# Attention sums over keys: from wide TensorE products to VectorE transpositions, and reciprocals broadcast through DRAM

## The chip, the cores and the metric

The kernel runs on one NeuronCore of one Trainium2 chip. The time is the device time of one execution in microseconds (us). Engines are named as in the profile: PE is TensorE (matrix products; PEld its weight loads), DVE is VectorE, ACT is ScalarE, POOL is GpSimd, SP is SyncE, which here only issues DMAs. A lower time is better.

## The reference

Four layers follow one another on x of shape (4, 512, 32, 32) in float32, each as x = x + f(group_norm(x)): an attention with mixed heads, a small simulated circuit that gates channels, an ordinary attention, and a lookup of the 8 best of 2048 memory rows. The change is in the third of them, layer 2:

```
q = conv1x1(x, Wq);  k, v = split(conv1x1(x, Wkv))        # 8 heads of 64 channels, 1024 positions
attn = softmax(einsum('bhct,bhcs->bhts', q, k) * 64**-0.5) # over the keys s
out  = conv1x1(einsum('bhts,bhcs->bhct', attn, v), Wp)
```

There are 4 images, so 4 x 8 heads x 1024 queries, each with a sum over 1024 keys. The kernel takes the softmax without subtracting a maximum, and so at its end it looks at a flag: if any reciprocal of a sum in layers 0 and 2 lay outside 1e-18 to 1e12, a second, general path computes everything anew.

## The kernel before

Layer 2 goes image by image. In an image, the eight heads are four pairs (m), the queries two halves of 512 (n), the keys eight tiles of 128. A *unit* is one pair of heads with one half of the queries; there are 8 an image, 32 in all. `UNITS2` lists half units (m, n, t0), t0 being 0 or 4, the first of four key tiles.

`scores2` computes a half unit. For each of four key tiles, PE multiplies keys and queries of the two heads (L1013) into a PSUM tile `sc` of 128 keys x 2 heads x 512 queries. ACT takes exp of it (L1007) into one of six places in `eT`. POOL adds pairs of these tiles (L1027 for the first pair, which starts the sum `es`; L1031 for the others), and DVE adds each such pair to `es` (L1032). `es` then holds, for 128 rests of the key index, partial sums over the eight tiles.

Between the second and the fourth exp, `scores2` calls `apply2` for the half unit before: PE multiplies values with the exponentials (L1046) and gathers the products of the eight tiles in a bank `pv`. Where `apply2` begins a unit (t0 == 0) it calls `finish2` for the unit that ended just before. `finish2` lets PE sum `es` over the partitions: two products of a matrix of ones with 512 columns, one for each head, which leave each sum in 64 partitions (L1067). ACT copies the result to SBUF (L1072), DVE takes 128x512 reciprocals (L1073) and multiplies `pv` by them into `o` (L1074). SP copies one row of reciprocals for each head into `seen` (L1077), which is looked at near the end (L1424).

At the end of an image the queries of the next image are projected, then the last half unit is applied, then the keys of the next image, then `finish2`, the values, the first scores of the next image, and `put_out2`, which projects `o` and adds x. After the last image comes one tile of layer 3's products (`attention`, L1134) in place of the next image's work.

PSUM has three `sc` buffers of two banks, which scores, small products and the sums of `finish2` take in turn, and two `pv` banks. Matrix products stand in program order (`pin`); instructions that aren't pinned are placed by the scheduler of the tile framework, each engine and each DMA queue then working in its own order.

Layer 0 has a similar step for its own sums (`sums`, L547 to L560): a product of a 128x128 matrix `same` with 32 columns of sums, a 128x32 reciprocal, two counting instructions into `seen0` (L552), a DMA of 32 rows to DRAM (`r_rows`, L556) and two DMAs from there, each broadcast to 64 partitions (L560).

Of the kernel before, what the change touches and what calls it, by code (L numbers as in the profile page):

```python
# [10 lines left out]
F32 = mybir.dt.float32  # L11
AF = mybir.ActivationFunctionType
ALU = mybir.AluOpType
AX = mybir.AxisListType
PSUM = bass.MemoryType.PSUM

P = 128
B = 4
C = 512
T = 1024  # L20
KC = C // P
TC = T // P
NB = 512
NH = 8
HD = C // NH
GSZ = C // 32
QB = 2
NQ = 9
# [8 lines left out]
R_LO, R_HI = 1e-18, 1e12  # L37
# [4 lines left out]
def fast_net(ctx: ExitStack, tc: tile.TileContext, a: dict, out: bass.AP, flag: bass.AP):  # L42
    nc = tc.nc
# [3 lines left out]
    const = ctx.enter_context(tc.tile_pool(name="const", bufs=1))  # L47
    small = ctx.enter_context(tc.tile_pool(name="small", bufs=4))
# [7 lines left out]
    def pin(ins):  # L56

        return tc.keep_in_program_order(ins)
# [5 lines left out]
    def chan(src, name):  # L64
# [11 lines left out]
    bp2 = chan(a["bp"], "bp2")  # L76
    fcb = chan(a["fc_b"], "fcb")

    both = const.tile([P, C], F32, tag="fcw", name="fcw")
    fcw, seen = both[0:NQ], both[HD:P]  # L80
    nc.scalar.dma_start(out=fcw, in_=a["fc_w"])
    qpar = const.tile([P, NL * NQ], F32, tag="qpar", name="qpar")
    nc.scalar.dma_start(out=qpar, in_=a["q_params"].partition_broadcast(P))
# [5 lines left out]
    ones = const.tile([P, P], F32, tag="ones", name="ones")  # L89
# [8 lines left out]
        out=gavg_v, in_=gavg_v, compare_op=ALU.is_ge, fill=0.0, base=0,  # L98
# [3 lines left out]
        out=gavg_v, in_=gavg_v, compare_op=ALU.is_ge, fill=0.0, base=GSZ - 1,  # L102
        pattern=[[GSZ, P // GSZ], [0, GSZ]], channel_multiplier=-1,
    )
    NS = 32
# [5 lines left out]
    same = const.tile([P, P], F32, tag="same", name="same")  # L111
# [119 lines left out]
    img = [dict() for _ in range(B)]  # L231
# [746 lines left out]
    def take_k2(b, m, at=None):  # L978
        I = img[b]
        if m == 0:  # L980
            I["k"] = big("k", f"k2_{b}")
        project(I["Wk"], tokens(I["xn"]), m, at, lambda ps: pin(nc.scalar.activation(
            I["k"][:, m, :], ps, AF.Identity, bias=bk2[:, m:m + 1])), f"k2_{b}")
# [11 lines left out]
    def scores2(b, u, before=None):  # L995

        m, n, t0 = u
        I = img[b]  # L1000
        nm = f"c{b}_{m}_{n}"
        es, scs = [], []

        def exp2():
            e = places2[:, count[0] % 6]
            count[0] += 1
            pin(nc.scalar.activation(e, scs[len(es)], AF.Exp))  # L1007
            es.append(e)

        for i, t in enumerate(range(t0, t0 + 4)):  # L1010
            sc = ps_s.tile([P, 2, NB], F32, tag="sc", name=f"sc_{nm}_{t}")
            for r in range(2):
                pin(nc.tensor.matmul(  # L1013
                    sc[:, r, :],
                    I["k"][r * HD:(r + 1) * HD, m, t * P:(t + 1) * P],
                    I["q"][r * HD:(r + 1) * HD, m, n * NB:(n + 1) * NB],
                    start=True, stop=True,
                ))
            scs.append(sc)
            if before is None or i < 2:  # L1020
                exp2()
        if before is not None:
            apply2(b, before, exp2)
        I["e", u] = list(es)
        if t0 == 0:
            I["es", m, n] = sums2[:, (2 * m + n) % 2]
            nc.gpsimd.tensor_add(I["es", m, n], es[0], es[1])  # L1027
            es = es[2:]
        for i in range(0, len(es), 2):
            two = pair_sum[:, (t0 + i) // 2 % 2]  # L1030
            nc.gpsimd.tensor_add(two, es[i], es[i + 1])  # L1031
            nc.vector.tensor_add(I["es", m, n], I["es", m, n], two)  # L1032

    def apply2(b, u, exp2=None):

        m, n, t0 = u
        I = img[b]
        if t0 == 0:
            finish2(b)
            I["pv", m, n] = ps_m.tile([P, NB], F32, tag="mm", name=f"pv_c{b}_{m}_{n}")  # L1040
        pv = I["pv", m, n]
        for i, e in enumerate(I.pop(("e", u))):
            t = t0 + i
            for r in range(2):
                h = 2 * m + r
                pin(nc.tensor.matmul(  # L1046
                    pv[r * HD:(r + 1) * HD, :], I["v"][:, t, h * HD:(h + 1) * HD],
                    e[:, r, :], start=(t == 0), stop=(t == TC - 1),
                ))
            if exp2 and i < 2:  # L1050
                exp2()
        if t0 == TC - 4:
            I["due"] = (m, n)

    def finish2(b):
        I = img[b]
        due = I.pop("due", None)
        if due is None:
            return
        m, n = due  # L1060
        nm = f"c{b}_{m}_{n}"
        if due == (0, 0):
            I["o"] = o_full.rearrange("p (k t) -> p k t", k=KC)
        es, pv = I.pop(("es", m, n)), I.pop(("pv", m, n))
        rsp = ps_s.tile([P, 2, NB], F32, tag="sc", name=f"rs_{nm}")[:, 0, :]
        for r in range(2):
            pin(nc.tensor.matmul(  # L1067
                rsp[r * HD:(r + 1) * HD, :], ones[:, 0:HD], es[:, r, :],
                start=True, stop=True,
            ))  # L1070
        ri = apool.tile([P, NB], F32, tag="rb", bufs=2, name=f"ri_{nm}")
        nc.scalar.copy(ri, rsp)  # L1072
        nc.vector.reciprocal(ri, ri)  # L1073
        nc.vector.tensor_mul(I["o"][:, m, n * NB:(n + 1) * NB], pv, ri)  # L1074
        for r in range(2):
            i = 2 * ((b * KC + m) * (T // NB) + n) + r
            nc.sync.dma_start(out=seen[i:i + 1, :], in_=ri[r * HD:r * HD + 1])  # L1077

    def put_out2(b):
        I = img[b]  # L1080
# [41 lines left out]
            ))  # L1122
            yield

    def attention(b, tt):

        nm = f"{b}_{tt}"
        att = eight_k([P, NI], f"att_{nm}")
        for half in range(2):
            sc = ps_s.tile([P, T], F32, tag="sc", name=f"at_{nm}_{half}")  # L1130
            for n in range(T // NB):
                i0 = half * T + n * NB
                for k in range(KC):
                    pin(nc.tensor.matmul(  # L1134
                        sc[:, n * NB:(n + 1) * NB],
                        xn3[b][:, k, tt * P:(tt + 1) * P], memT[k][:, i0:i0 + NB],
                        start=(k == 0), stop=(k == KC - 1),
                    ))
            pin(nc.scalar.copy(att[:, half * T:(half + 1) * T], sc))  # L1139
        return att  # L1140

    def pick(b, tt, att):
# [212 lines left out]
    for k in range(KC):  # L1355
        if k < 2:
            m_ = apool.tile([P, NI], F32, tag="s2", bufs=2, name=f"memT{k}")
        else:
            m_ = eT_flat[:, (4 + k) * NI:(5 + k) * NI]
        nc.sync.dma_start(out=m_, in_=a["memT"][k * P:(k + 1) * P, :])  # L1360
        memT.append(m_)
    tiles = [(b, tt) for b in range(B) for tt in range(TC)]
    atts, picks, sums = {}, {}, {}
    scores2(0, UNITS2[0])
    for b in range(B):
        last = b + 1 == B
        behind = chain(
            behind if b else state["behind"], norm3(b - 1) if b > 0 else gating(B - 1))
        ahead = prepare3(0) if last else prepare2(b + 1)
        for s, u in enumerate(UNITS2):  # L1370
            if s == 5 and not last:
                load2(b + 1)
            if s == 5 and last:
                img[b]["Wp"] = load_w("Wp", f"Wp2_{b}")
            if s >= 1:
                scores2(b, u, UNITS2[s - 1])
            for _ in range(2):
                if s >= 3:
                    next(behind, None)
                if s >= 8:  # L1380
                    next(ahead, None)
        run_out(ahead)
        if not last:
            for m in range(KC):
                take_q2(b + 1, m)
            img[b]["Wp"] = load_w("Wp", f"Wp2_{b}")
        apply2(b, UNITS2[-1])
        if not last:
            for m in range(KC):
                take_k2(b + 1, m)  # L1390
        finish2(b)
        if last:
            atts[0] = attention(*tiles[0])
        else:
            for i in range(TC // 2):
                take_v2(b + 1, i)
            scores2(b + 1, UNITS2[0])
        put_out2(b)
# [18 lines left out]
            next(behind, None)  # L1417


    counts = small.tile([P, 3], F32, tag="counts", name="counts")  # L1420
    nc.vector.memset(counts, 0.0)
    passed = apool.tile([P, NB], F32, tag="xr", bufs=2, name="passed")[HD:P]
    for i, (bound, op) in enumerate(((R_LO, ALU.is_ge), (R_HI, ALU.is_le))):
        nc.vector.tensor_scalar(  # L1424
            passed, seen, bound, None, op, ALU.add, accum_out=counts[HD:P, i:i + 1]
        )
    nc.vector.tensor_reduce(counts[:, 2:3], seen0, AX.X, ALU.add)
    tot = small.tile([P, 1], F32, tag="tot", name="tot")
    nc.vector.tensor_reduce(tot, counts, AX.X, ALU.add)
    tps = ps_m.tile([P, NB], F32, tag="mm", name="tot")  # L1430
    nc.tensor.matmul(tps[:, 0:1], ones, tot, start=True, stop=True)
    nc.vector.tensor_scalar(
        flag, tps[0:1, 0:1], float(2 * HD * NB + 2 * P * NS * B * TC), None, ALU.not_equal)


@with_exitstack
# [702 lines left out]
```

## Time and profile before

| what | value |
| --- | --- |
| median of 3 runs | 2636.74 us (2635.33 to 2646.7) |
| profiled execution: its own time, and its span | 2636.8 us, 2635.1 us |
| PE, DVE, POOL, ACT busy | 97%, 57%, 45%, 38% of the span |
| sums over keys on PE (L1067) | 128 records, about 604 ns each (they overlap) |
| ACT copies of the sums (L1072) | 32 of 0.586 us |
| reciprocals (L1073) | 32 of 3.346 us |
| multiplications by them (L1074) | 32 of about 0.68 us |
| pair sums on POOL (L1031) | 96 of 2.414 us |
| adds of pair sums on DVE (L1032) | 96 of 1.315 us |

A row such as `L1073 DVE RECIPROCAL ri_c<-ri_c 128x512 f32<-128x512 f32` names the line, the engine, the operation, the tile written and the tile read (shared buffers have the name of the first tile in them, so `eT` stands for several), and their shapes. A float32 product appears as two records, and records of PE overlap, so their durations don't add up; the distance between starts does. What stands in brackets at the end of a timeline row is how long the engine was idle before it, and what released it.

### The profile page before, as it was taken

Reading aid. Unit: us, or ns where it says so; the run is one execution under the profiler, and the core shown is the slowest. Engines: PE = TensorE matmul, PEld = TensorE weight load, DVE = VectorE, ACT = ScalarE, POOL = GpSimd, SP = SyncE. Lnnn points to the kernel's source line nnn. Section 1 sums busy time; section 2 is a strip of 40 time slices with the busy share of each in tenths; the row PEclk is TensorE's granted clock in tenths of the full one; section 3 lists DMA queues with packets and bytes.
Section 4 is the critical chain, followed back from the end, with each engine's and each line's share of the span. In section 5 each row is a group of like instructions: output and inputs, shape, how many; then the busy total and the mean of one; then the engine's idle time right before and its main releaser. Section 6 shows DMA issues by size and latency. Waiting matters only on the chain.

```text
span 2635.1 us, 47129 instructions
## 1 busy us (share of the span) xinstructions
PE 2553.4 (97%) x18350; PEld 1158.9 (44%) x18350; DVE 1498.8 (57%) x2451; ACT 997.3 (38%) x1148; POOL 1196.3 (45%) x1699
## 2 busy tenths in 40 slices
PE   8999999999999999999999999999999999999995
PEld 3344434554355534545533433443343344444442
DVE  4499338970789338871354145234413547788786
ACT  1566236651666236651252145025314622121210
POOL 2266315552456425552283056017404617656664
PEclk9999999999999999999999999999999999999997
DMA  2478439871698338793300220030012036767665
GB/s 81 129 218 236 107 101 228 251 201 54 176 256 243 104 96 222 226 248 120 128 1 17 71 73 1 32 128 1 1 53 75 1 100 184 221 183 219 187 181 156
DMA packets 182360, 349.82 MB, mean 133 GB/s; under 512 B 32361, under 2 KB 95849, under 8 KB 178418
## 3 DMA queue, kind: packets, MB, share of 16 engines
q1 hardware_dynamic: 100896, 167.17, 21.0%
q0 software_dynamic: 49152, 142.79, 19.9%
q10 hardware_dynamic: 32082, 36.76, 5.2%
q8 instruction: 148, 2.42, 0.4%
q14 instruction: 82, 0.67, 0.1%
HBM read 178.57 MB, written 33.69 MB: 81 GB/s over the span
## 4 chain that ended last, share of the span: by engine, by line
PE 87%; DMA 6%; DVE 3%; ACT 2%; issue 1%; SPq 1%; POOL 0%; ACTq 0%; POOLq 0%; DVEq 0%
PE at L1134 17%; PE pair L193 10%; PE sc_c L1013 9%; PE pv_c L1046 9%; PE pv L523 7%; PE pair L458 6%; PE pair L484 5%; PE pt L417 4%; DMA s<-ss 4%; PE p L193 3%; PE pt L711 3%; PE k L193 3%; PE v L205 3%; PE q L193 3%; ACT e L491 1%; PE rs_c L1067 1%
## 5 line engine op out<-in xcount | busy, mean ns | idle before, releaser
L473 POOL DMA_DIRECT2D s<-ss x512 | 258.9, 512 | 456.8 <-PE pair L484 154.9
L497 DVE STREAM_TRANSPOSE eT<-e 128x1024 f32<-128x1024 f32 x256 | 316.4, 1236 | 206.0 <-ACT e L491 205.6
L1151 POOL DMA_INDIRECT got<-in_mem,ix x256 | 277.9, 1086 | 217.5 <-DVE tmx L1157 94.3
L512 DVE BATCH_NORM_STATS2 st<-e 128x6 f32<-128x256 f32 x1024 | 350.4, 403 | 6.2 <-POOL sqs L571 6.2
L1007 ACT ACTIVATE eT<-sc_c 128x1024 f32<-128x1024 f32 x256 | 247.7, 1022 | 276.0 <-PE sc_c L1013 213.8
L491 ACT ACTIVATE e<-pair 128x1024 f32<-128x1024 f32 x256 | 251.7, 1022 | 187.9 <-PE pair L484 136.2
L1031 POOL TENSOR_TENSOR e<-eT 128x1024 f32<-128x1024 f32 x96 | 231.7, 2414 | 179.2 <-ACT eT L1007 153.9
L464 ACT COPY ss<-pair 128x1024 f32<-128x1024 f32 x256 | 247.3, 1019 | 87.4 <-PE pair L458 43.2
L458 PE MATMUL pair<-k,q 64*32 64x512 f32 x4096 | 265.1, 598 | 11.8 <-ACT e L491 11.8
L1032 DVE TENSOR_TENSOR eT<-eT,e 128x1024 f32<-128x1024 f32 x96 | 126.3, 1315 | 247.5 <-POOL e L1031 247.2
L523 PE MATMUL pv<-eT,v 128*64 128x128 f32 x4096 | 252.0, 276 | 5.9 <-ACT pv L583 5.9
L523 PEld LDWEIGHTS pv<-eT,v 128*64 128x64 f32 x4096 | 222.2, 137 | 76.1 <-issue 56.9
L1013 PE MATMUL sc_c<-q,k 64*128 64x512 f32 x1024 | 237.2, 602 | 2.6 <-DVE xr L674 2.3
L1027 POOL TENSOR_TENSOR eT<-eT 128x1024 f32<-128x1024 f32 x32 | 81.0, 2533 | 344.4 <-ACT eT L1007 334.2
L1046 PE MATMUL pv_c<-eT,v 128*64 128x512 f32 x1024 | 232.2, 596 | 0.0
L484 PE MATMUL pair<-s,wmix 32*32 32x512 f32 x4096 | 159.7, 606 | 14.8 <-DMA s<-ss 8.9
L1175 DVE SCALAR_TENSOR_TENSOR acc<-got,et,acc 128x512 f32<-128x512 f32 x224 | 168.5, 752 | 8.0
L1073 DVE RECIPROCAL ri_c<-ri_c 128x512 f32<-128x512 f32 x32 | 107.1, 3346 | 96.1 <-ACT ri_c L1072 96.1
L1013 PEld LDWEIGHTS sc_c<-q,k 64*128 64x128 f32 x1024 | 93.5, 186 | 131.8 <-issue 72.0
L1139 ACT COPY att<-at 128x1024 f32<-128x1024 f32 x64 | 64.8, 1012 | 216.6 <-PE at L1134 216.5
L1046 PEld LDWEIGHTS pv_c<-eT,v 128*64 128x64 f32 x1024 | 70.3, 137 | 152.8 <-issue 152.2
L458 PEld LDWEIGHTS pair<-k,q 64*32 64x32 f32 x4096 | 57.6, 105 | 172.9 <-ACT e L491 79.5
(290 smaller groups left out, 3279.5 us busy)
## 6 DMA issues: line engine op xcount, KB each, us to landing
s<-ss SPq DMA_DIRECT2D x512, 128.0 KB
s<-ss POOLq DMA_DIRECT2D x512, 128.0 KB, 4.8
rb<-r POOLq DMA_DIRECT2D x64, 128.0 KB, 6.6
o<-o SPq DMA_DIRECT2D x32, 256.0 KB
xr<-in_x ACTq DMA_DIRECT2D x32, 256.0 KB
x<-xr SPq DMA_DIRECT2D x32, 256.0 KB
xr_c<-x SPq DMA_DIRECT2D x32, 256.0 KB
x<-xr_c SPq DMA_DIRECT2D x32, 256.0 KB
```

The source lines that it names most:

```text
L193: pin(nc.tensor.matmul(ps[:, n, :], w[:, k, m * P:(m + 1) * P], rhs(k, n), start=(k == 0), stop=(k == KC - 1),))
L458: pin(nc.tensor.matmul(sc[m * NS:(m + 1) * NS, r, :], q[r * HD:(r + 1) * HD, m, s * NS:(s + 1) * NS], k_[r * HD:(r + 1) * HD, m, n * NB:(n ...
L473: pin(relays[side].dma_start(out=s2[2 * m + r::NH], in_=ss[m * NS:(m + 1) * NS, r, :]))
L484: pin(nc.tensor.matmul(mixed(s, r // 2)[t * NS:(t + 1) * NS, r % 2, :].rearrange("p (qq k) -> p qq k", qq=2), wmix[r * NS:(r + 1) * NS], s ...
L491: pin(nc.scalar.activation(e[:, half].rearrange("p r qq k -> p (r qq k)"), flat2(mixed(s, half)), AF.Exp))
L497: pin(nc.vector.transpose(eT[:, j % 2].rearrange("p b (qq i r) x -> p i r qq b x", qq=2, i=4)[:, i, 2 * half:2 * half + 2], e[:, half].rea ...
L512: pin(nc.vector.bn_stats(st[:, i, 2 * half + r, qq, :], e[:, half, r, qq, :]))
L523: pin(nc.tensor.matmul(pv[r * HD:(r + 1) * HD, gp, :], I["v"][:, t, g * HD:(g + 1) * HD], eT[:, j % 2, t, :, 4 * g:4 * g + 4], start=(t == ...
L1013: pin(nc.tensor.matmul(sc[:, r, :], I["k"][r * HD:(r + 1) * HD, m, t * P:(t + 1) * P], I["q"][r * HD:(r + 1) * HD, m, n * NB:(n + 1) * NB] ...
L1046: pin(nc.tensor.matmul(pv[r * HD:(r + 1) * HD, :], I["v"][:, t, h * HD:(h + 1) * HD], e[:, r, :], start=(t == 0), stop=(t == TC - 1),))
L1134: pin(nc.tensor.matmul(sc[:, n * NB:(n + 1) * NB], xn3[b][:, k, tt * P:(tt + 1) * P], memT[k][:, i0:i0 + NB], start=(k == 0), stop=(k == K ...
L1151: pin(nc.gpsimd.indirect_dma_start(out=got[:, i, :], out_offset=None, in_=a["mem"], in_offset=bass.IndirectOffsetOnAxis(ap=ix[:, i:i + 1], ...
```

## The change

The sum over the 128 partitions is moved from PE mostly to DVE. When a unit's `es` is complete (at the end of `scores2`, t0 == 4), the new `over_keys` turns `es` in blocks of 32x32 (two transpositions of 128x512) and adds 32 neighbours (two reductions to 128x16). What remains, a sum over four groups of partitions, is made by two small products with `same`, which was layer 0's matrix and is scaled by POOL once. They stand in `invert2`, at the place where `finish2` stood. `invert2` also takes 128x32 reciprocals straight from PSUM, turns them, counts them into `seen0`, and sends them through DRAM, on POOL's queue, to a 128x512 tile `rb`. `finish2` is now only the multiplication of `pv` by `rb`, and stands half a unit later. At an image's end, `invert2` comes after the first of the four key projections; after the last image, between the two halves of the first `attention` tile. The tile `seen`, its DMAs and its counting go.

```diff
@@ scores2
+        if t0 == TC - 4:
+            over_keys(b, m, n)
@@ apply2
         if t0 == 0:
+            invert2(b)
+            I["pv", m, n] = ps_m.tile([P, NB], F32, tag="mm", name=f"pv_c{b}_{m}_{n}")
+        else:
             finish2(b)
-            I["pv", m, n] = ps_m.tile([P, NB], F32, tag="mm", name=f"pv_c{b}_{m}_{n}")
@@
+    def over_keys(b, m, n):
+        I = img[b]
+        es = I.pop(("es", m, n))
+        s_ = I["s", m, n] = small.tile([P, 2, NB // NS], F32, tag="sums", name=f"s_c{b}_{m}_{n}")
+        for r, tag in enumerate(("o1", "xs")):
+            turned = apool.tile([P, NB], F32, tag=tag, name=f"est_{b}_{m}_{n}_{r}")
+            nc.vector.transpose(turned, es[:, r, :])
+            nc.vector.tensor_reduce(
+                s_[:, r, :], turned.rearrange("p (q x) -> p q x", x=NS), AX.X, ALU.add)
+
+    def invert2(b):
...
+        m, n = I["ready"] = due
+        ps = ps_s.tile([P, 2, NB], F32, tag="sc", name=f"rs_{nm}")[:, 0, 0:NS]
+        s_ = I.pop(("s", m, n)).rearrange("p r q -> p (r q)")
+        for half in range(2):
+            pin(nc.tensor.matmul(
+                ps[half * HD:(half + 1) * HD], same[:, half * HD:(half + 1) * HD], s_,
+                start=True, stop=True))
+        ri = small.tile([P, NS], F32, tag="ri", name=f"ri_c{nm}")
+        nc.vector.reciprocal(ri, ps)
+        ris = small.tile([P, NS], F32, tag="ssq", name=f"ris_{nm}")
+        nc.vector.transpose(ris, ri)
+        for bound, op in ((R_LO, ALU.is_ge), (R_HI, ALU.is_le)):
+            nc.vector.scalar_tensor_tensor(seen0, ri, bound, seen0, op, ALU.add)
+        rows = r_rows[n % 2]
+        nc.gpsimd.dma_start(out=rows, in_=ris[0:NS])
+        rb = I["rb", m, n] = apool.tile([P, NB], F32, tag="rb", bufs=2, name=f"rb_c{nm}")
+        for r in range(2):
+            nc.gpsimd.dma_start(
+                out=rb[r * HD:(r + 1) * HD],
+                in_=rows.rearrange("(r q) x -> r (q x)", r=2)[r].partition_broadcast(HD))
+
     def finish2(b):
...
-        for r in range(2):
-            pin(nc.tensor.matmul(
-                rsp[r * HD:(r + 1) * HD, :], ones[:, 0:HD], es[:, r, :],
-                start=True, stop=True,
-            ))
-        ri = apool.tile([P, NB], F32, tag="rb", bufs=2, name=f"ri_{nm}")
-        nc.scalar.copy(ri, rsp)
-        nc.vector.reciprocal(ri, ri)
-        nc.vector.tensor_mul(I["o"][:, m, n * NB:(n + 1) * NB], pv, ri)
-        for r in range(2):
-            i = 2 * ((b * KC + m) * (T // NB) + n) + r
-            nc.sync.dma_start(out=seen[i:i + 1, :], in_=ri[r * HD:r * HD + 1])
+        nc.vector.tensor_mul(
+            I["o"][:, m, n * NB:(n + 1) * NB], I.pop(("pv", m, n)), I.pop(("rb", m, n)))
@@ before layer 2
+    nc.gpsimd.tensor_scalar_mul(same, same, 8.0 / T)
@@ at the end of an image
             for m in range(KC):
                 take_k2(b + 1, m)
+                if m == 0:
+                    invert2(b)
+        if last:
+            atts[0] = attention(*tiles[0], lambda: invert2(b))
         finish2(b)
@@ at the end
-        nc.vector.tensor_scalar(
-            passed, seen, bound, None, op, ALU.add, accum_out=counts[HD:P, i:i + 1]
-        )
...
-        flag, tps[0:1, 0:1], float(2 * HD * NB + 2 * P * NS * B * TC), None, ALU.not_equal)
+        flag, tps[0:1, 0:1], float(2 * P * NS * B * (TC + 2 * KC)), None, ALU.not_equal)
```

## The prediction

> **What bounds the kernel now.** I read the page first: its busy shares, and the chain that ended last, by engine and by line.
>
> ```profile
> span 2635.1 us, 47129 instructions
> PE 2553.4 (97%) x18350; PEld 1158.9 (44%) x18350; DVE 1498.8 (57%) x2451; ACT 997.3 (38%) x1148; POOL 1196.3 (45%) x1699
> ...
> PE 87%; DMA 6%; DVE 3%; ACT 2%; issue 1%; SPq 1%; POOL 0%; ACTq 0%; POOLq 0%; DVEq 0%
> ```
>
> TensorE is the bound over the whole span, so an edit is worth what it takes from or adds to PE's row of products. Layer 2 runs from about 1290 to 2163 us. Table of windows there, in stretches of one unit (15.5 us): PE is busy 15.50 in nearly every one, DVE 5 to 13, ACT 8.5, POOL 9.4 to 14.3, at a granted clock of 1.00; DMA is 0.00 to 0.01 while units run. Next the chain in order of time, where the products stand one after the other (start, us, what):
>
> ```profile
> 1303.41 3.63 PE sc_c L1013 x16
> 1307.05 3.58 PE pv_c L1046 x16
> 1310.63 3.63 PE sc_c L1013 x16
> 1314.27 1.01 PE rs_c L1067 x4
> 1315.27 3.43 PE pv_c L1046 x16
> ...
> 1330.57 3.43 PE pv_c L1046 x16
> 1334.00 0.32 PE gps_b L146 x2
> ```
>
> A unit is twice (scores, values); the sums over keys, rs_c, come in the middle and take 1.01. The values product takes 3.58 where the scores follow, 3.43 where something else does: a change of operand form costs 0.15. So rs_c is worth 1.01 - 0.15 = 0.86 us a unit. The timeline of one unit shows the side engines (start, busy us, engine, line):
>
> ```profile
> 2097.23 2.36 POOL L1031 TENSOR_TENSOR e<-eT 128x1024 f32<-128x1024 f32 x1 [1.40 <-DVE eT L1032]
> 2097.49 1.08 PE L1067 MATMUL rs_c<-eT,ones 128*64 128x512 f32 x4
> ...
> 2099.63 1.23 DVE L1032 TENSOR_TENSOR eT<-eT,e 128x1024 f32<-128x1024 f32 x1 [2.54 <-POOL e L1031]
> 2100.77 3.35 DVE L1073 RECIPROCAL ri_c<-ri_c 128x512 f32<-128x512 f32 x1
> 2101.56 2.34 POOL L1031 TENSOR_TENSOR e<-eT 128x1024 f32<-128x1024 f32 x1 [1.96 <-ACT eT L1007]
> ```
>
> Below, t is counted from this rs_c (2097.49). On PE: values at t = 0.9, scores 4.5, values 8.1, scores 11.7, next rs_c 15.3.
>
> **Removed.** All 32 units lose their wide sums: 32 x 0.86 = 27.5 us of PE, all on the path. VectorE loses the wide reciprocal (3.35 each), ScalarE the copy L1072 (0.59 each), SP the 64 DMAs L1077. None of these is on the chain, so they are worth 0; also 0 for the counting at L1424 (two of 0.68, at 2170 us, while PE runs layer 3 without a gap).
>
> **Added on TensorE.** Two small products a unit: the 128x32 sums, as moving data, against 64 columns of `same` each, four records. The nearest row is layer 0's product with the same matrix and as many columns, in the timeline there:
>
> ```profile
> 812.09 0.41 PE L547 MATMUL pt<-sums,same 128*128 128x32 f32 x2
> ...
> 812.43 1.97 PE L523 MATMUL pv<-eT,v 128*64 128x128 f32 x32
> ```
>
> It holds the row for 812.43 - 812.09 = 0.34. Two half-width products lie side by side as rs_c's two did, so I take one such price: 0.34 - 0.15 = 0.19 a unit, 32 x 0.19 = 6.1 us. Bounds: L438 (1x64 weights) passes 32 records in 1.02 us, so four cost 0.13, which the change of form hides: 0. If the two halves go one after the other, 2 x 0.34 - 0.15 = 0.53, or 17.0 in all. So PE gains 27.5 - 6.1 = 21.4, between 10.5 and 27.5.
>
> The Trainium skill (TensorE: Matmul & The Clock Gate, "Wait — 56ns, not 53.3ns?") says that starts of products never come closer than about 25 ns, however few columns. By it alone four records would need an estimated 0.10 us, and the gain would be near the upper bound.
>
> **Added on VectorE.** Two 128x512 transpositions, half of L497's 1.236 each, 0.62; two reductions, half of the 1.209 at L843, 0.60; a 128x32 reciprocal, 0.34 (L550); a 128x32 transposition, bounded by L635's 0.14 and L550's 0.34; two counting instructions, 0.19 (L552). Sum 3.4, against 3.35 removed: VectorE is as full as before. What changes is order. The built order is: add (pair 4), reciprocal, turn, count, add (pair 6), two transpositions, two reductions, multiplication of the unit before, then the next unit's adds.
>
> **Added on GpSimd.** One DMA issue of 0.52 (L556) and two of 0.64 (L560): 1.80 a unit. The first stands between its two adds and waits for the turned reciprocals; the second pair waits until the first has landed; behind them stands the next unit's first add. POOL goes from 9.4 to 11.2 in a plain unit of now 14.6 and stays off the path.
>
> **The new waits, in one unit.** Reciprocal after the add that ends at t = 3.4, so 3.4 to 3.75, turned by 4.0; first DMA issued 4.05; POOL's add, formerly at 4.07, at 4.6 to 6.95. VectorE's add 7.0 to 8.2, transpositions and reductions to 10.7. The price of the trip through DRAM depends on how full the DMA is. In layer 0 it is full, and the tile's median to landing is 6.2 and 6.6. But layer 2's units are quiet, and layer 0 has a quiet stretch too (889 to 922 us, DMA share 0.17), which shows:
>
> ```profile
> DMA to landing us min/median/max: 2.9/3.0/4.2
> ```
>
> I take 3.0 for each hop: written at 7.05, the two broadcasts issued to 8.35, landed at 10.7, so just about when VectorE gets to the multiplication: 10.7 to 11.4. The value bank is wanted again at the unit's end, 15.0 by the new row: 3.6 us spare. The sums are ready at 10.7 for a product at 14.6: 3.9 spare. The PSUM buffer of the small product is wanted by the third score tile at about 5.6 and is free at 3.75, as no ScalarE copy but VectorE frees it: 1.9 spare, the tightest. So a plain unit has no new stall.
>
> It is gone where VectorE or POOL lags. In images 0, 1 and 2, four normalizations (L961, 1.5 to 1.8 each) fall in one unit: there the multiplication ends at 14.7 and the reciprocal at 6.4 after its product, 0.8 too late for the buffer: about 1 us in each of three images. In image 0, POOL is busy 13.9 and 14.3 of 15.5 with the gate's small work (1341 to 1372); plus 1.8 it is late by about a microsecond there. At the end of the last image the two hops stand between the halves of an attention tile: 6.9 us of the second half and 6.0 of the projection cover some 9; at busy-DMA prices 2.6 would show. Together I take 3 us; 0 to 10.
>
> One rule speaks against the change. The two counting instructions read two SBUF operands. By the Trainium skill (SBUF — State Buffer, "Who interferes with whom") such an instruction and a GpSimd one that reads SBUF exclude each other for their whole length, while one-input instructions do not. The rows agree: L1032 takes 1.23 mostly but 3.17 at 1337.77 under a POOL add, and L552 takes 0.19 mostly but 1.43 at worst. By the rule each unit could lose an estimated 2.4 on VectorE, not on PE. I price them at their median, as POOL then issues its DMA.
>
> **The sum**, against the profiled execution's own time, 2636.8 (span 2635.1 and 1.7 around it; the median of the runs is 2636.74, the same): 2636.8 - 21.4 + 3 = 2618.4.
>
> **Rivals.**
> - *The gain is eaten but not turned.* The small products cost their upper price (gain 10.5), or the three late places grow to 10 us: 2636.8 - 10.5 + 3 = 2629, or 2636.8 - 21.4 + 10 = 2625. For it: POOL's 14.3 plus 1.8 exceeds a unit in image 0, and PE's small forms have irregular prices (gate L903: 8 records in 0.98). Against: only two or three units are so full. 2624 to 2636.
> - *Slower: the trip through DRAM sets the end of each unit.* VectorE stands at the multiplication until the broadcast has landed, and the value bank comes free after PE wants it. It decides when the two hops take more than about 9.5 us together: 4.05 + hop + 0.65 + hop + 0.8 = 15.0. At layer 0's medians (6.2 + 6.6 = 12.8) each of 28 inner units would stall 3.3: 2636.8 - 21.4 + 92 = 2707. For it: those medians come from 32 and 64 issues, the quiet value from three. Against: DMA share of 0.01 where units run.
> - *The change does not do what it says.* If the count compared at the end came out wrong, the general path would run, by milliseconds. The written constant, 2 x 128 x 32 x 4 x (8 + 8), matches 32 + 32 groups counted twice, so this gets little.
>
> **How the numbers follow.** A measurement of this kernel can tell about 0.5%, 13.2 us, from no change: faster is below 2623.5, slower above 2649.9. The forecast (2611 to 2623.5) gets 0.64, the eaten gain 0.20, the slow trip 0.14, the wrong count 0.02. The range takes the forecast and the eaten gain: 2611, near the upper bound of the gain less the 3 given back, to 2636; it leaves out the slow cases and a little below. Faster 0.64, same 0.20, slower 0.16.
>
> **What would show it.** Right: the chain has scores, about 0.34 for the small products, values, and a plain unit of 14.6 instead of 15.3; PE still busy all of layer 2; hops of about 3 us. Wrong: PE waiting for VectorE's reciprocal or multiplication in most units; hops of 5 us or more; four small records holding PE for 0.6 or more; POOL without idle time through layer 2.

## The result, and the profile after

The change made the kernel slower: 2672.16 us (median of 4, 2663.56 to 2678.87) against 2636.97 us for the kernel before. The ratio is 1.0122, with a 95% interval of 1.0097 to 1.0147. A second set of runs of both kernels gave 2671.56 against 2640.32, 1.0119 (1.0102 to 1.0136). The profiled execution took 2663.56 us, its span 2661.8.

The page of the changed kernel, its busy shares and the chain that ended last:

```profile
span 2661.8 us, 47226 instructions
PE 2543.7 (96%) x18350; PEld 1160.6 (44%) x18350; DVE 1522.7 (57%) x2669; ACT 980.1 (37%) x1116; POOL 1236.7 (46%) x1796
...
PE 74%; DVE 9%; POOL 7%; DMA 5%; ACT 2%; issue 2%; SPq 1%; ACTq 0%; POOLq 0%; DVEq 0%
```

PE's busy time fell by 10 us while the span grew by 27. PE's share of the chain fell from 87 to 74%; DVE rose from 3 to 9% and POOL from 0 to 7%. So something that VectorE and GpSimd pass to each other now sets part of the end. In this pair of profiles, layer 2, from its first score to the end of its last projection, takes 896.5 us instead of 870.4; what lies behind it takes 470.5 instead of 472.0. What lies ahead of it differs by 2.0. Two windows over layer 2, first of the profile before, then of this one, and a third over a short stretch inside it (start and end, length, busy us and number of instructions of PE, PEld, DVE, ACT and POOL, granted clock, DMA share, GB/s):

```profile
1292.70:2163.10 870.40, 870.16 (x3099) 339.90 (x3100) 338.15 (x278) 312.63 (x357) 350.14 (x221) 1.00 0.12 41
1294.70:2191.20 896.50, 857.18 (x3099) 339.30 (x3100) 362.68 (x503) 295.00 (x326) 391.85 (x317) 0.99 0.15 50
1339.60:1343.00 3.40, 3.40 (x10) 1.39 (x8) 0.68 (x1) 1.33 (x2) 2.66 (x2) 0.50 0.01 1
```

So PE, which was idle for 0.2 us of the old layer 2, now stands idle for 39.3 of it. And in five stretches of 3.4 us, the one shown among them, its granted clock is halved, where it was 1.00 throughout before.

The waits of layer 2 (engine, line, what it waited for: us in total, times, longest):

```profile
POOL r L1090 <- DVE seen L1088: 171.6, 32, 35.2
...
PEld sc_c L1012 <- DVE ri_c L1084: 39.5, 16, 5.0
POOL e L1030 <- DVE eT L1031: 37.8, 20, 3.6
...
PE sc_c L1012 <- DVE ri_c L1084: 25.4, 15, 4.1
DVE eT L1105 <- DMA rb_c<-r: 23.8, 6, 5.4
```

PE waits for the reciprocal, ri_c: with the 25.4 of its row above and five smaller ones, it does so for 35.7 of the 39.3 us. In the profile of before PE had no wait for it at all: there the copy of the sums out of PSUM was ScalarE's, not VectorE's. The broadcast rows (rb_c) keep VectorE waiting in only six units of 32. The timeline of one unit of image 3, in which no other work stands (start, us, engine, line, what; in brackets the idle time before and its releaser):

```profile
2093.68 0.31 PE L1080 MATMUL rs<-s_c,same 128*64 128x32 f32 x4
2093.83 3.65 PE L1049 MATMUL pv_c<-eT,v 128*64 128x512 f32 x16
2098.99 3.71 PE L1012 MATMUL sc_c<-q,k 64*128 64x512 f32 x16 [1.51 <-DVE ri_c L1084]
```

Two things are to be read here. First, the *first* score product after the small product stands still, from 2097.48, which is t = 3.8 after the small product; the prediction had the third score tile need that PSUM buffer, at about 5.6. Second, the reciprocal ends only at t = 5.3, where the prediction had 3.75. Why it is so late is in the chain in order of time, over the same unit (start, us, what):

```profile
2083.13 0.20 DVE seen L1088
2083.33 0.50 POOL r L1090
...
2083.86 2.38 POOL e L1030
...
2086.26 4.43 DVE eT L1031
...
2090.71 1.30 DVE est L1065 x2
...
2093.18 0.60 DVE eT L1105
2093.77 1.14 DVE eT L1031
...
2095.08 2.34 POOL e L1030
...
2097.44 1.23 DVE eT L1031
2098.67 0.28 DVE ri_c L1084
...
2099.29 0.20 DVE seen L1088
```

From one counting to the next it is 16.16 us, and no PE stands in it. It is a closed loop: VectorE's counting releases POOL's issue of the first transfer; behind that issue stands POOL's last addition of the unit; VectorE's last add comes after it and takes 4.43 instead of 1.23; transpositions, reductions and the multiplication follow, then VectorE's add of the next unit; POOL's next pair sum waits for that add, because both write and read the same pair buffer (`(t0 + i) // 2 % 2` gives the buffer 0 to the second and the third pair); then VectorE's add, the reciprocal, the counting. PE's own work for a unit is 14.6, so it waits 1.5. The 4.43 is explained by what POOL does beside it:

```profile
2086.15 1.05 POOL L1093 DMA_DIRECT2D rb_c<-r  x2
2086.26 4.42 DVE L1031 TENSOR_TENSOR eT<-eT,e 128x1024 f32<-128x1024 f32 x1 [2.94 <-POOL e L1030]
...
2087.21 2.37 POOL L1026 TENSOR_TENSOR eT<-eT 128x1024 f32<-128x1024 f32 x1
```

VectorE's add ends 1.10 after POOL's addition of the next unit (2089.58): it ran behind it, not beside it, although it had started 0.95 earlier. In the profile of before POOL paused at this place, and VectorE's add was done when POOL's first addition of the next unit began:

```profile
2104.03 1.16 DVE L1032 TENSOR_TENSOR eT<-eT,e 128x1024 f32<-128x1024 f32 x1
...
2105.19 2.37 POOL L1027 TENSOR_TENSOR eT<-eT 128x1024 f32<-128x1024 f32 x1 [1.29 <-DVE eT L1032]
```

### The profile page after: what moved, and what is told of

It is laid out like the page before. It is cut to its first block, busy times and chain, and to the rows that moved or that the text cites. A ratio compares the mean times of both kernels' runs of the same rounds, so it can differ in the third digit from the quotient of the medians.

```text
span 2661.8 us, 47226 instructions
## 1 busy us (share of the span) xinstructions
PE 2543.7 (96%) x18350; PEld 1160.6 (44%) x18350; DVE 1522.7 (57%) x2669; ACT 980.1 (37%) x1116; POOL 1236.7 (46%) x1796
## 4 chain that ended last, share of the span: by engine, by line
PE 74%; DVE 9%; POOL 7%; DMA 5%; ACT 2%; issue 2%; SPq 1%; ACTq 0%; POOLq 0%; DVEq 0%
PE at L1163 17%; PE pair L192 10%; PE pv L522 7%; PE pair L457 6%; PE pair L483 5%; POOL e L1030 5%; PE pt L416 4%; DVE eT L1031 4%; PE p L192 4%; PE pt L710 3%; PE k L192 3%; PE q L192 3%; DMA s<-ss 3%; PE v L204 3%; PE sc_c L1012 2%; PE pv_c L1049 2%
## 5 line engine op out<-in xcount | busy, mean ns | idle before, releaser
L1031 DVE TENSOR_TENSOR eT<-eT,e 128x1024 f32<-128x1024 f32 x96 | 153.7, 1601 | 250.0 <-POOL e L1030 249.9
L1012 PE MATMUL sc_c<-q,k 64*128 64x512 f32 x1024 | 245.3, 620 | 28.5 <-DVE ri_c L1084 25.4
L1163 PE MATMUL at<-memT,xn_d 128*128 128x512 f32 x256 | 120.7, 594 | 0.0
```

What stands on the lines that cost most here:

```text
L1012: pin(nc.tensor.matmul(sc[:, r, :], I["k"][r * HD:(r + 1) * HD, m, t * P:(t + 1) * P], I["q"][r * HD:(r + 1) * HD, m, n * NB:(n + 1) * NB] ...
L1163: pin(nc.tensor.matmul(sc[:, n * NB:(n + 1) * NB], xn3[b][:, k, tt * P:(tt + 1) * P], memT[k][:, i0:i0 + NB], start=(k == 0), stop=(k == K ...
```

## Experiments

The theory after this look had two parts: a loop over VectorE and POOL in the plain units (those without other work), and a PSUM tile that only VectorE frees. Each edit is against the changed kernel unless said. The times from one small product to the next (start to start on PE) for the last, plain units of image 3 and for the long units, the length of layer 2, and the ratio to the kernel before on the same chip:

| kernel | plain unit, us | longest unit, us | layer 2, us | ratio (95%) |
| --- | --- | --- | --- | --- |
| before | 15.3 | 17.1 | 870.4 | 1 |
| the change | 16.2 | 21.4 | 896.5 | 1.0122 (1.0097 to 1.0147) |
| SyncE issues all three transfers | 14.6 | 22.1 | 882.9 | 1.0065 (1.0048 to 1.0082) |
| SyncE issues only the first | 14.6 | 22.7 | 882.8 | 1.0077 (1.0051 to 1.0103) |
| SyncE issues only the broadcasts | 15.1 | 22.2 | 888.1 | 1.0075 (1.0058 to 1.0092) |
| broadcasts issued later by POOL | 15.1 | 23.5 | 894.1 | 1.0098 (1.0081 to 1.0114) |
| pair buffers in turn | 15.6 | 21.9 | 890.7 | 1.0079 (1.0061 to 1.0097) |
| ScalarE's copy | 14.6 to 18.1 | 22.8 | 910.3 | 1.0179 (1.0144 to 1.0214) |
| copy, and buffers in turn | 14.6 to 18.0 | 23.1 | 906.1 | 1.0161 (1.0143 to 1.0180) |
| SyncE, and copy | 14.6 | 19.0 | 856.3 | 0.9961 (0.9947 to 0.9974) |
| SyncE, copy, and buffers in turn | 14.6 | 18.3 | 854.4 | 0.9947 (0.9930 to 0.9965) |
| before, its copy left out | 15.8 | 23.0 | 911.6 | 1.0148 (1.0125 to 1.0171) |

**SyncE issues the three transfers.**

```diff
-        nc.gpsimd.dma_start(out=rows, in_=ris[0:NS])
+        nc.sync.dma_start(out=rows, in_=ris[0:NS])
...
-            nc.gpsimd.dma_start(
+            nc.sync.dma_start(
```

> The three DMAs of each unit (rows to DRAM, two broadcasts back) are issued by SP instead of GpSimd; nothing else differs from the changed kernel. Theory P (port and loop): in the changed kernel the add of the last pair finds GpSimd issuing the broadcasts and then starting the next unit's first add, so it takes 4.4 us instead of 1.23, and the adds of both engines form a closed loop of 16.2 us a unit. Without GpSimd's issues the add takes 1.23 again, the loop is about 12.5 us, PE sets the unit at 14.6, and the time is 2614 to 2624. Rival B (bank: only the late reading of the small product's PSUM tile stops PE): the order on VectorE is the same, so 2655 to 2680. Rival D (the trip through DRAM is too long): issued from SP the trip is at most half a microsecond shorter, 2650 to 2680.

Measured: 2657.66 us against 2641.54, far above the 2614 to 2624 of theory P. What it said of the plain units held: they fell to 14.6, PE's own time, so the loop goes through POOL's issues. But five units of 19.6 to 22.1 stayed, three of them in image 0. The timeline of one of them:

```profile
1375.53 0.31 PE L1080 MATMUL rs<-s_c,same 128*64 128x32 f32 x4
...
1376.77 4.66 POOL L1030 TENSOR_TENSOR e<-eT 128x1024 f32<-128x1024 f32 x2
...
1379.16 3.35 DVE L1031 TENSOR_TENSOR eT<-eT,e 128x1024 f32<-128x1024 f32 x1 [4.74 <-POOL e L1030]
1382.43 0.34 DVE L1084 RECIPROCAL ri_c<-rs 128x32 f32<-128x32 f32 x1
...
1382.92 0.34 PE L890 MATMUL z<-pr,signs 128*9 128x1 f32 x8 [3.62 <-DVE ri_c L1084]
```

Small work for the gate had held POOL until 1376.77; then it makes two pair sums without a pause. VectorE's add of the first of them takes 3.35 beside the second, and the reciprocal stands behind that add, at t = 6.9. Whatever PE would put into the next buffer waits 3.6. This is the second part of the theory.

**Pair buffers strictly in turn.**

```diff
-            two = pair_sum[:, (t0 + i) // 2 % 2]
+            two = pair_sum[:, pairs_used[0] % 2]
+            pairs_used[0] += 1
```

> The two buffers of pair sums are taken strictly in turn (a running count), so GpSimd's sum of the third pair no longer waits for VectorE's add of the second. Theory P: the long add of 4.4 us stays, but the loop loses GpSimd's 2.4 us wait, from 16.2 to about 13.8, under PE's 14.6: 2614 to 2630. Rival B: the reciprocal still comes late in VectorE's row, behind the add of the third pair, which now ends about 1 to 2 us earlier; part of the loss goes: 2635 to 2655. Rival D: no change, 2655 to 2680.

Measured: 2663.69, so theory P's 2614 to 2630 was wrong and the time lies in the range of rival D. Plain units of 15.6: the shared buffer closes the loop of 16.2, but without it PE still waits. What holds these units at 15.6 was not followed further.

**ScalarE's copy.**

```diff
-        nc.vector.reciprocal(ri, ps)
+        nc.scalar.copy(ri, ps)
+        nc.vector.reciprocal(ri, ri)
```

> ScalarE copies the 128x32 result of the small product to SBUF, and VectorE takes the reciprocal there: the PSUM tile comes free as early as before the change. Theory P: the loop of 16.2 us does not pass through PSUM, so PE then waits at another place, and the time stays at 2650 to 2675. Rival B: PE's waits for the reciprocal, 1.5 us a unit, go altogether: 2612 to 2624. Rival D: 2655 to 2680.

Measured: 2682.82, worse than the change itself and above all three ranges. PE no longer waits for the reciprocal, so it comes earlier to the next small product, and waits there for the sums. The timeline:

```profile
2085.90 1.06 POOL L1094 DMA_DIRECT2D rb_c<-r  x2
2086.01 6.74 DVE L1031 TENSOR_TENSOR eT<-eT,e 128x1024 f32<-128x1024 f32 x1 [3.04 <-POOL e L1030]
...
2095.39 0.43 PE L1080 MATMUL rs<-s_c,same 128*64 128x32 f32 x4 [3.47 <-DVE s_c L1066]
```

VectorE's last add takes 6.74, in eight units 6.7 to 7.0: as PE runs ahead, the exponentials are ready earlier, and POOL makes two additions behind its issues without a pause (2086.98 and 2089.28); VectorE's add runs after both. So freeing PE sharpened the other conflict. Yet PE's idle time in layer 2 rose only from 39.3 to 42.5 us. Most of the 13.8 that layer 2 grew is the granted clock: it was halved in five stretches of 3.4 us and four of 6.8, one of them beginning in the wait shown:

```profile
2094.90:2101.70 6.80, 6.23 (x18) 2.04 (x20) 4.04 (x8) 2.23 (x3) 2.52 (x2) 0.50 0.00 0
```

**The broadcasts issued after the next unit's first addition, by POOL.** In this kernel `spread2` issues the two broadcasts and `finish2` multiplies. The last but one unit of each image, (3, 0), stays without both.

```diff
-            nc.gpsimd.tensor_add(I["es", m, n], es[0], es[1])
+            pin(nc.gpsimd.tensor_add(I["es", m, n], es[0], es[1]))
+            spread2(b)
+            finish2(b)
...
-        else:
-            finish2(b)
...
```

> GpSimd issues the two broadcasts after the first add of the next unit instead of before it; the same number of issues on the same engine, and the multiplication comes some 2 us later. Theory P: what counts is that an issue of GpSimd no longer stands ready when VectorE's add of the last pair starts; that add takes 1.23 again in the units in which the next exponentials are not ready by then, and the time falls to 2616 to 2640. Rival B: 2655 to 2680. Rival D: the trip ends later, so slower than the changed kernel, 2675 to 2710.

Measured: 2668.0, in the range of rival B. Plain units of 15.1; VectorE's last add takes 3.37 in place of 4.43, since POOL's next addition starts beside it all the same, 0.09 ahead of it (2094.12 and 2094.21). VectorE waits 68.7 us for the broadcast rows in 15 units, as they are issued later; little of this reaches PE.

**Both causes removed: SyncE issues, ScalarE copies.** The edits of the first and the third experiment together.

> The change with two edits at once: SyncE issues the three transfers of a unit instead of POOL, and ScalarE copies the small product's result from PSUM to SBUF before VectorE takes the reciprocal. Theory of two causes (the plain units' loop over VectorE and POOL goes with POOL's transfer issues, and the long units of 19 to 22 us go when the PSUM tile no longer waits for VectorE's reciprocal): with the first edit alone ten long units stood 5 to 7 us over a plain one's 14.6; about 2 us of each stay, so layer 2 shrinks from 882.9 to 840-862 us and the whole time is 2612-2636, faster than before the change. No wait of PE for the reciprocal is left. Rival 1, one cause (the late POOL addition itself holds the sums, and with them the small product, however the tile is freed): the long units stay at 19 us or more, PE's wait moves to the small product or to pv's bank, 2650-2662. Rival 2 (the copy costs ScalarE's exponentials as much as it frees): plain units go back above 15.2 and the time is 2640-2665.

Measured: 2629.23 (12 runs, 2624.36 to 2638.79) against 2640.3. The largest waits of PE's products that are left in layer 2:

```profile
PE rs L1080 <- DVE s_c L1066: 3.5, 1, 3.5
PE sc_c L1012 <- DVE xr L673: 2.3, 1, 2.3
PE sc_c L1012 <- DVE xr_c L1121: 1.0, 1, 1.0
```

No wait for the reciprocal remains, and of the long units (five in the first experiment, not the ten of the expectation) only those of 17.2 and 19.0 in image 0. The edits work in full only together: against the change, SyncE alone takes 13.6 us off layer 2, the copy alone adds 13.8, both take off 40.2. The theory of two causes holds; both rivals fall.

**All three edits.**

> The kernel of the run before with a third edit: the sums of two key tiles go strictly in turn into the two pair buffers, so that a POOL addition waits for VectorE's second last one and not for its last. Theory of two causes: plain units already stand at PE's own 14.6, so only units in which VectorE is late can gain, at most 2 us in each of some eight: 2606-2636, within 16 us below the run before. Rival (the shared buffer is itself what makes the long units, because POOL stands behind VectorE's late addition there too): the long units fall by 3 us or more only here, 20-35 us less than the run before.

Measured: 2626.28 (6 runs), 0.9947 of before. It is the fastest kernel of this study, faster than both others, but its interval overlaps that of the run before it, and layer 2 differs by 1.9 us: the third edit can't be told from nothing here. The long units fall by at most 0.7, so the rival falls.

**The old kernel without its copy.** This asks whether the PSUM tile alone has such a price, without POOL's transfers and without the new sums.

```diff
-        nc.scalar.copy(ri, rsp)
-        nc.vector.reciprocal(ri, ri)
+        nc.vector.reciprocal(ri, rsp)
```

> The kernel before the change with one edit: ScalarE's copy of the broadcast sums out of PSUM is left out, and VectorE's reciprocal of 128x512 reads PSUM itself. All else, the products with ones among it, stays. Theory that PE's wait comes from a PSUM tile that is held until VectorE's reciprocal has run: the tile is now held for 3.4 us and whatever stands before it on VectorE, against 1.7 us from the product to the end of the copy before; a unit grows by 1 to 4 us over 15.3, layer 2 by 30-110 us, 2665-2750, with PE waiting for VectorE's reciprocal in nearly every unit. Rival (the tile is not what binds; only POOL's transfer issues are): no unit of layer 2 changes by over 0.3 us, 2628-2650.

Measured: 2680.83, 1.0148 of before; layer 2 grew by 41.2. Its waits on PE in layer 2:

```profile
PE sc_c L1013 <- DVE ri_c L1072: 25.9, 23, 5.0
```

So the copy was worth 41 us to the old kernel, though it was on no chain and no wait showed it. Of these, 26.7 are idle time of PE, and an estimated 8.5 stretches of halved clock behind it; about 6 remain unexplained. The prediction had priced the copy's removal at 0.

**Copy and turn, with POOL still issuing; and the change again.**

> The change with ScalarE's copy of the small product and with the pair buffers strictly in turn; POOL goes on issuing the three transfers. Theory (POOL's issues followed by its additions without a gap keep VectorE's last addition from running, 6.7 us for one of 1.2 where the copy was added alone, so the sums and the next small product are late): as long as POOL issues, units of 16 to 21 us remain and PE waits for the small product's sums, layer 2 880-910 us, 2650-2690. Rival (the pair buffer that two additions share closes the loop, and the transfer issues only fill time that POOL has): with copy and turn the units go to 14.6-15.3 as they did when SyncE issued, layer 2 852-868 us, 2622-2640.

> The changed kernel itself on the chip of the run before, to set the single edits against it: 2660-2680 and a ratio of 1.009 to 1.015 by every theory; layer 2 890-900 us. If the start of layer 2 differs from 1294.7 by several us, what lies ahead of it varies from run to run and is no part of the change.

Measured: 2682.22 and 2671.56 against 2640.32. With copy and turn, PE waits for the small product's sums as before (25.1 us in 7 waits), and units of 17 to 18 remain, so the shared buffer isn't the rest of the loop: POOL's transfers are. The change's own second profile has layer 2 at 899.4, its start at 1301.1 instead of 1294.7.

**Which of POOL's issues.** Two kernels, with one half each of the first experiment's edit.

> The change with SyncE issuing only the first of a unit's three transfers, the write of 32 rows, which waits for VectorE's counting; POOL still issues the two broadcasts. Theory W (what matters is that POOL stands between its two additions and waits for VectorE's reciprocal and counting, 171.6 us in 32 waits, so that its last addition comes late and the next unit's first one follows without a gap): the plain units fall from 16.2 to 14.6-14.9, the long units of 18 to 22 stay because the PSUM tile still waits for VectorE; 2650-2664. Theory I (the two broadcasts, 1.05 us of issue ahead of the next unit's first addition, are what sets it against VectorE's last addition): the plain units stay at 15.8-16.2 and VectorE's last addition at 4.4; 2664-2674.

> The complement: SyncE issues the two broadcasts, POOL the first write, with its wait. Theory W: POOL's last addition is as late as before, the next unit's first one now follows it at once, VectorE's last addition takes 3.4 in place of 4.4 and the plain units stand at 15.0-16.0; 2660-2672. Theory I: plain units at 14.6, VectorE's last addition at 1.2; 2650-2660.

Measured: 2659.94 and 2665.21 against 2644.18. The whole times can't be told apart, but the units can: 14.6 where POOL no longer issues the first transfer, 15.1 where it no longer issues the broadcasts. The timeline of the kernel in which POOL issues the broadcasts only:

```profile
2076.33 2.34 POOL L1030 TENSOR_TENSOR e<-eT 128x1024 f32<-128x1024 f32 x1 [1.23 <-ACT eT L1006]
...
2078.77 1.06 POOL L1093 DMA_DIRECT2D rb_c<-r  x2
2078.87 1.22 DVE L1031 TENSOR_TENSOR eT<-eT,e 128x1024 f32<-128x1024 f32 x1
2079.97 2.36 POOL L1026 TENSOR_TENSOR eT<-eT 128x1024 f32<-128x1024 f32 x1
```

and of its complement:

```profile
2088.17 0.52 POOL L1090 DMA_DIRECT2D r<-ris  x1 [2.07 <-DVE seen L1088]
2088.71 2.37 POOL L1030 TENSOR_TENSOR e<-eT 128x1024 f32<-128x1024 f32 x1
2091.01 2.37 POOL L1026 TENSOR_TENSOR eT<-eT 128x1024 f32<-128x1024 f32 x1
2091.11 3.36 DVE L1031 TENSOR_TENSOR eT<-eT,e 128x1024 f32<-128x1024 f32 x1 [2.93 <-POOL e L1030]
```

In the first, POOL's last pair sum waits only for an exponential, and VectorE's add fits beside the issue of the broadcasts: 1.22. In the second, POOL's last pair sum stands behind the first issue, which waits for the counting; it comes so late that the next unit's first addition follows it at once, and VectorE's add loses to that one. So it isn't the 1.57 us that POOL spends on issuing. It is where its queue waits for `seen`, 2.06 to 2.49 in each of the 28 units inside the images, and what stands behind. (The other 113 of the 171.6 us are the four waits at the images' ends.)

## The prediction, step by step

**Right.** PE's gain was sized well. Where nothing holds PE (SyncE and copy), a plain unit takes 14.6, as forecast. From start to start the small products hold the row for 0.13 there (2064.02 to 2064.15), where 0.34 was taken from layer 0's row, and the values behind them take 3.57. In the profile of before the wide sums held it for 0.91 and the values behind them took 3.53 (starts at 2082.20, 2083.11 and 2086.64). So a unit saves 0.91 + 3.53 - 0.13 - 3.57 = 0.74 rather than 0.67. The 0.15 for a change of operand form came from the chain, which divides the same 4.44 into 1.01 and 3.43; by starts, 3.53 stands against 3.58 behind scores, so it is 0.05. The 0.86 of the wide sums is the same either way. VectorE's additions to its work came to 1.30 + 1.24 + 0.35 + 0.21 + 0.38 = 3.48 (forecast 3.4), POOL's issues to 0.52 + 1.05 = 1.57 (forecast 1.80), and the two hops through DRAM to 1.6 and 2.8 at the median, where 3.0 each was forecast. The second is in the row of issues of the changed kernel's page (KB each, us to landing):

```profile
rb_c<-r POOLq DMA_DIRECT2D x64, 128.0 KB, 2.8
```

**Wrong, and first in order: "The PSUM buffer of the small product is wanted by the third score tile at about 5.6 ... 1.9 spare".** The first score product waits for it, at t = 3.8. The tile order was taken from a strict turn of three buffers and not read from the changed program's waits. Why the first product waits there, and not the third, stays open. With the reciprocal done at 3.75 the spare was 0.05, not 1.9. The prediction called this cover the tightest, and named that "no ScalarE copy but VectorE frees it"; it nevertheless priced the copy's removal at 0. In the old kernel that removal costs layer 2 41.2 us.

**Wrong, and decisive in plain units: "So a plain unit has no new stall".** Two steps of the reasoning led there. The one was "POOL goes from 9.4 to 11.2 in a plain unit of now 14.6 and stays off the path": a sum of busy times, where the order on the queue decides. POOL's issue waits for VectorE's counting, POOL's last pair sum waits behind it, and VectorE needs that sum. The prediction wrote each of these down ("The first stands between its two adds", "behind them stands the next unit's first add") but followed them once, from t = 0, and not round to the next unit, where the reciprocal's own place depends on them. It also took "the add that ends at t = 3.4" from the old timeline; in the loop that add ended at t = 5.0. In a line shown there, POOL's pair sum at 2097.23 waits for VectorE's add of the pair before; that link was not used. The other was VectorE's add, taken at 1.23 throughout.

**The rule on the shared port was applied to the wrong instructions.** The Trainium skill (SBUF — State Buffer, "Who interferes with whom") lets a two-operand VectorE instruction and a GpSimd one that reads SBUF exclude each other for their whole length. The prediction priced it for the two counting instructions only. In the changed kernel these took 0.19 at most, as POOL was waiting for them. It was VectorE's adds, which also have two operands, that lost: ten of 96 took 4.4 us, two 3.2 and 3.4, together 36 us above 1.22, where the profile of before has five of 3.2 to 3.4, 10 us. With SyncE issuing, POOL no longer waits, and the counting does lose: in the kernel with SyncE and copy two instructions take 2.17 (2067.80) instead of 0.38, which PE does not notice there. The other half of the prediction's sentence on this, that one-input instructions do not lose, the page states only outside the modes that use both ports; in the profile of before, five of the twelve normalizations at L961, with one tensor input, took 2.4 to 2.9 instead of 0.8 beside a POOL addition.

**Mis-sized: the units with other work.** "Together I take 3 us; 0 to 10" is the term of the sum that failed: in layer 2 it measured 47.5, plain units included. "About 1 us in each of three images" and "late by about a microsecond" in image 0 were 4 to 7 us above PE's 14.6, where the old kernel's stood up to 1.8 above its 15.3: the sixth units of images 0 to 2 take 20.8, 20.1 and 18.6, and units 2 and 4 of image 0 take 19.1 and 21.4. In four of these five a stretch of halved clock, an estimated 1.7 us, is part of it; the prediction read a granted clock of 1.00 and had no term for losing it.

**The rivals.** The kernel became slower, but not by the rival that said so: VectorE waited for the broadcast in six units, not in 28. The rival that came nearest in words, "the three late places grow", had the mechanism of the long units and no room for a loop in the plain ones. Among the signs that would make it wrong the prediction listed "PE waiting for VectorE's reciprocal or multiplication in most units"; that is what came.

**The account.** Forecast -21.4 + 3. Layer 2 can be split into PE's idle time, what the halved clock cost (an estimate: half of PE's busy time in those stretches), and the rest, which is PE's work at the full clock:

| kernel | work | halved clock | idle | layer 2, us |
| --- | --- | --- | --- | --- |
| before | 870.2 | 0 | 0.2 | 870.4 |
| the change | 848.8 | 8.4 | 39.3 | 896.5 |
| SyncE issues all three | 847.1 | 10.4 | 25.3 | 882.9 |
| ScalarE's copy | 848.7 | 19.2 | 42.5 | 910.3 |
| SyncE, and copy | 847.0 | 3.2 | 6.1 | 856.3 |
| before, its copy left out | 876.2 | 8.5 | 26.9 | 911.6 |

PE's work fell by the 21.4 of the forecast. That it agrees to the tenth is luck: the small products were priced too high, and 32 x 0.74 would be 23.7. Against it stand 39.1 more of idle time and 8.4 of halved clock, 47.5 in place of 3, which makes +26.1. Removing both causes takes back 40.2: 33.2 of idle time, 5.2 of halved clock and 1.8 of work. What the copy alone adds to the change, 13.8, is about 3.2 of idle time and 10.8 of halved clock, so its harm is mostly the clock. Its waits of PE are longer, up to 6.2 us against 4.1. The medians differ by 35.2; in the first pair of profiles layer 2 has 26.1 of it, in the second profile 29.0. The rest lies ahead of layer 2, where the order on PE and on SyncE is the same and a few instructions on the other engines differ: its start varies from 1292.7 to 1310.8 among the profiles of all these kernels, in stretches with full DMA queues. Why it is mostly later than in the one profile of before stays open; the fastest kernel here starts layer 2 at 1304.3.

## What to carry to other kernels

A copy that frees a PSUM tile can look free to remove, as it is on no chain and nobody waits for it; ask who frees the tile then, what stands ahead of that instruction on its queue, and read from the built program's waits which product takes the tile next. A DMA issue that waits is a wait for everything behind it on its engine, so add up the order on the queue and not the busy times, and follow it round to the next pass of the loop. When two suspected causes stand in one loop, remove them together as well as singly: here one edit took 14 us off the layer, the other alone added 14, and both together took off 40. Look at the granted clock too before a longer time is put down to a conflict: most of the 14 that the one edit added were halved clock.

## What the runs showed of the hardware

Which of VectorE's add and POOL's addition runs first, where they overlap, is shown by all thirteen profiles together. With no DMA issue of POOL beside it, the earlier start decided: 229 adds began 0.02 to 1.23 ahead of a large addition of POOL, and all took 1.23 or less, as at 1640.81 with SyncE issuing, where POOL's addition began 0.92 later and took 2.52 instead of 2.37. Three adds that began 0.08 to 0.13 ahead lost; in each a small POOL instruction stood beside it.

A POOL DMA issue beside it did not by itself hold the add. Beside 1.06 of issue, where POOL's addition came 1.1 to 1.2 after the add's start, it took 1.22 or 1.23 in eleven places of twelve, as at 2078.87. (In the twelfth, 1326.88 with ScalarE's copy, a small POOL instruction stood directly behind the issue, and the add took 6.97.) But where POOL's addition followed the issue at once, 0.94 to 1.00 after the add's start, the add lost its head start in 48 of 54 places and ended 1.1 behind POOL's addition, or behind two of them. In the six others it took 1.23 and POOL's addition 2.45 to 2.52, as at 2134.78 in the changed kernel. What decides between the two was not tried.

PE's granted clock in layer 2 was 1.00 or 0.50 in every profile, and a long wait of PE can cost more than its length. The profile of before has none at 0.50 there; the other twelve have 57 such stretches, of 3.4 or 6.8 us. Each began 1.7 to 5.4 us after the start of a wait of PE of 1.97 us or more, and none behind waits of 1.9 or less alone, such as the 1.5 of the plain units; 15 waits of 2.3 to 3.4 in the thirteen profiles had none behind them. That the waits set it off is read from this order and was not tried.

From start to start, four small products of 32 columns hold PE's row for 0.13, and 3.57 follows for the values where 3.53 followed behind 512 columns; the layer 0 row of 0.34, with full 128-column weights ahead of products of 128 columns, was a poor neighbour.
